# Layer norm roots of a gated FFN kernel split between VectorE and GpSimd, with two moved weight loads and a regrouped LoRA merge

## The chip, the cores and the metric

The kernel runs on 1 core of one Trainium2 chip. The metric is device time in microseconds (us) of one execution. Before the change the median of 3 runs is 442.76 us, from 442.38 to 443.26 us.

## What is computed

The input `u` is 2 x 1024 rows (tokens) of 512 floats; everything is fp32. Each row is normalised (mean and variance over its 512 columns), goes through a state-space convolution over those columns and through a gated FFN with LoRA corrections, and the two results are multiplied and added to the row:

```
def _layernorm(x, axis=-1, eps=1e-05):
    m = jnp.mean(x, axis=axis, keepdims=True)
    v = jnp.var(x, axis=axis, keepdims=True)
    return (x - m) / jnp.sqrt(v + eps)
...
    h1 = _lora_linear(x, w1, lora_A1, lora_B1)
    h3 = _lora_linear(x, w3, lora_A3, lora_B3)
    g = jax.nn.silu(h1) * h3
    return _lora_linear(g, w2, lora_A2, lora_B2)
...
x = L0_attn_u
xn = _layernorm(x, axis=-1)
s = _L0_attn_ref(xn, ...)
g = _silu(_L0_ffn_ref(xn, ...))
x = x + s * g
```

`_lora_linear(x, w, a, b)` is `x w^T + 2 (x a^T) b^T` with rank 16; `w1` and `w3` are 1376 x 512, `w2` is 512 x 1376. Only the layer norm and the first stretch of the first two products (`w1`, `w3`) matter for this change.

## The kernel before

**Blocks.** The 2048 rows are 4 blocks of 512 rows, each of 4 tiles of 128 rows x 512 columns. `load_x` requests the tiles, `norm_stats` takes mean and variance of a tile on VectorE (DVE; `bn_stats` and `bn_aggr`, L247 and L248), `norm_root` computes 1/sqrt(variance + eps) for all tiles of one or two blocks with ten small DVE instructions on a [128, n] tile (L281, the eight of `rsqrt`, L57 to L66, and L284), and `normalize` applies it, one tile after the other, on ScalarE (ACT, L293) or GpSimd (POOL, L297). The tiles are then transposed on TensorE (PE, `transpose`, L304), and ACT copies the results from PSUM into `xr` and `b12` (L312, L314, L315). For block 3 mean and variance come from ACT sums (`act_sums`, `act_squares`, L254 and L265) with small POOL instructions behind them (L260, L261, L274).

**Products.** The products with `w1` and `w3` are done by a scheme of seven products in place of eight, twice nested: on the outside over block pairs, so sums of transposed blocks (`outer_token_sum`, L328, into `xt`) and sums of weights (`outer_weight_sums`, L440) are operands as well. A `Chain` (L765) is seven such products, steps 1, 2, 7, 6, 5, 3, 4. Steps 1, 6, 5 and 3 add into one PSUM bank `x`; after steps 6 and 5 ACT copies the state of that bank away (`snapshot`, L775), and the next step may add to the bank only after the copy. All matmuls of a chain are at L755 (`product`).

The first chain is that of the last 96 hidden rows (`last_chain`, weights `w_last`, tile `last`); the second, beside it, is the first of weight pair 0 (`pair_chain(0, 0)`, weights `w_pair[0]`, tile `w`). Their steps are placed by hand on one time axis with `at(place, what)`; a heap of these events is emptied in order of place, and each engine then runs its own instructions in exactly the order in which they were recorded. So an engine's order is fixed, and an instruction that waits holds everything behind it on its engine. The steps of the first two chains stand at

```
add_chain(0, lambda: last_chain(ab_last, 0),
    ((1, -11), (2, -8), (7, -2), (6, 1.6), (5, 5.6), (3, 8.6), (4, 11.6)))
add_chain(0, pair_chain(0, 0),
    ((1, -4), (2, -1.8), (7, 3.6), (6, 4.6), (5, 7.6), (3, 10.6), (4, 13.6)))
```

**LoRA.** The LoRA term is folded into the weights: `lora_product` (L382) makes a block of it in PSUM by a matmul over 16 rows, `merge` (L392) adds it to the weights on DVE. The LoRA factors lie in groups of 32 partitions of one tile pair (`lo_d`, `lo_h`). `merge_pair` uses groups 0 and 1 and makes four products in two banks, for one half of a pair; it is called twice for pair 0. `merge_whole_pair` uses the four groups and makes all eight products in four banks at once; before the change it serves the later pairs only. The factors of groups 2 and 3 are four small loads (L371, L372).

**Transfers.** All loads except four of the first go out on the sync engine's queue (SP), in program order; a load waits until the one eight places before it has landed. The order is: tiles of block 0, first LoRA factors, block 1, `w1` and `w3` of the last rows (L469), pair 0 (L401), blocks 2 and 3, pair 1, LoRA factors of groups 2 and 3.

**Head and tail.** Before the event list runs, the code records the head: 20 idle matmuls on an identity (`keep_warm`, L990), the LoRA products of the last rows, statistics, root and normalisation of block 0, 5 and 2 more idle matmuls around the transposes of block 0, statistics and root of block 1, and the merges of the last rows. In the list, `normalize(1)` stands at -10, its transposes at -6 and -5, `norm_stats` of block 2 from -6 to -3.6, the root of blocks 2 and 3 at 6.9, `normalize(2)` at 7.3, `normalize(3)` at 7.4, and the transposes of blocks 2 and 3 from 12.1.

Of the kernel before, what the change touches and what calls it, by code (L numbers as in the profile page):

```python
# [17 lines left out]
P = 128  # L18
# [31 lines left out]
def rsqrt(nc, pool, v, shape):  # L50
# [15 lines left out]
    nc.vector.scalar_tensor_tensor(y, t, 5.0, y, ALU.add, ALU.mult)  # L66
    return y
# [40 lines left out]
def s4_gated_ffn(  # L108
# [169 lines left out]
    def norm_root(mv, *blocks):  # L278
        n = len(blocks) * NTT
# [5 lines left out]
        for n, b in enumerate(blocks):  # L285
            norms[b] = [t[:, n * NTT : (n + 1) * NTT] for t in (rstd, shift)]
# [12 lines left out]
    def transpose(b, tiles, tag="aux"):  # L299
        sb, low = divmod(b, 2)  # L300
        for tt in tiles:
            ps = bank(tag)
# [104 lines left out]
    def merge_pair(c, w, half, tag="aux"):  # L407

        ps = [bank(tag), bank(tag)]
        for k in range(2):  # L410
            for v in range(2):
                n = slice(k * 2 * P, (k + 1) * 2 * P)
                lora_product(ps[v][:, n], v, 2 * half + k, PAIR_AT[c], 2 * P, k == 0)
        for v in range(2):
            to = w[:, (1, 2, 0, 3)[2 * v + half]].rearrange("p k m h -> p (k m h)")
            after(1.6 + v, lambda to=to, v=v: merge(to, ps[v]))

# [44 lines left out]
    def load_last():  # L462
# [5 lines left out]
        for v, src in enumerate((w1T, w3T)):  # L468
            nc.sync.dma_start(  # L469
                out=w[:, v], in_=src[:, LAST * P :].rearrange("(dc p) h -> p dc h", p=P)  # L470
            )
        return w, s
# [499 lines left out]
    nc.scalar.activation(warm, warm, AF.Silu)  # L972
    x_in[1] = load_x(1)
    make_upper_triangular(nc, tri, 1.0, diag=True)
    w_last, s_last = load_last()
# [3 lines left out]
    for v, f in enumerate(factors):  # L979
        load_lora(nc.sync, 2 + v, *f, LSPLIT, HID)  # L980
# [19 lines left out]
    for ps in primed:  # L1000
        keep_warm(ps, 10, True)
    ps_last = lora_last()
    mv = norm_tile(0)
    norm_stats(0, range(NTT))
    norm_root(mv, 0)
    normalize(0)

    for i in range(2):
        keep_warm(primed[1], (5, 2)[i])
        transpose(0, range(2 * i, 2 * i + 2))  # L1010
    mv = norm_tile(1)
    norm_stats(1, range(2))
    merge_last(w_last, ps_last, 0)
    norm_stats(1, range(2, NTT))
    norm_root(mv, 1)
    merge_last(w_last, ps_last, 1)
# [41 lines left out]
    at(-10, lambda: normalize(1))  # L1058
# [3 lines left out]
    for i in range(2):  # L1062
        at(-6 + i, lambda i=i: transpose(1, range(2 * i, 2 * i + 2), "y"))
# [529 lines left out]
```

## Time and profile before

| what | us |
|---|---|
| median of 3 runs | 442.76 |
| the profiled execution, its own time | 442.51 |
| its span, first to last instruction | 440.7 |
| PE busy in the span | 434.7 (99%) |
| DVE busy | 315.0 (71%) |
| ACT busy | 144.6 (33%) |
| POOL busy | 209.3 (47%) |

The time holds 1.8 us that lie outside the span (442.51 - 440.7). PE is busy nearly throughout, but its busy time is a model and contains idle matmuls and short waits in the head. The stretches of 5 us from the start show where the engines stand (busy time and, in brackets, the number of instructions):

| stretch | PE | DVE | ACT | POOL | GB/s of DMA |
|---|---|---|---|---|---|
| 0 to 5 | 3.63 (17) | 0.98 (3) | 1.49 (2) | 1.15 (9) | 222 |
| 5 to 10 | 5.00 (43) | 4.31 (17) | 0.34 (1) | 0.28 (1) | 285 |
| 10 to 15 | 5.00 (38) | 4.10 (14) | 3.39 (6) | 1.24 (2) | 349 |
| 15 to 20 | 4.70 (27) | 4.73 (15) | 3.40 (8) | 3.78 (6) | 377 |
| 20 to 25 | 5.00 (21) | 4.33 (9) | 4.49 (14) | 0.36 (2) | 262 |
| 25 to 30 | 4.87 (12) | 4.97 (9) | 4.39 (11) | 0.35 (2) | 10 |
| 30 to 35 | 4.86 (25) | 3.76 (15) | 3.54 (6) | 2.89 (4) | 39 |
| 35 to 40 | 5.00 (24) | 4.96 (7) | 2.60 (6) | 2.25 (4) | 41 |

### The profile page before, as it was taken

How to read it: one execution, taken by the hardware profiler on the slowest of the kernel's cores; microseconds unless marked ns; L12 is line 12 of the kernel's file. 1: busy time of each engine (PE TensorE's matmuls, PEld its weight loads, DVE VectorE, ACT ScalarE, POOL GpSimd, SP SyncE). 2: the span in 40 equal slices, each digit the busy share in tenths (PEclk: the TensorE clock that was granted, in tenths of full speed). 3: DMA queues.
4: the chain of work that ended last, by engine and by line, in shares of the span. 5: the costliest groups of instructions: out<-in, count | busy, mean ns of one | idle time of the engine just before them, and what ended most of it. 6: DMA issues, size and time to landing. Idle time of an engine off the chain costs nothing.

```text
span 440.7 us, 5176 instructions
## 1 busy us (share of the span) xinstructions
PE 434.7 (99%) x1714; PEld 270.7 (61%) x1714; DVE 315.0 (71%) x534; ACT 144.6 (33%) x296; POOL 209.3 (47%) x156
## 2 busy tenths in 40 slices
PE   8999999999999999999999999999999999999996
PEld 8635334444444444444443446888898999999995
DVE  5899999946874687458745796979786885653234
ACT  2776342553245324532453242211101212212221
POOL 2316469995689458936894469400000122222221
PEclk9999999999999999999999999999999999999999
DMA  8921304025002400250045527395901833432211
GB/s 254 369 64 48 123 0 149 24 74 167 25 24 87 153 24 25 92 166 24 25 136 199 162 88 220 98 362 190 348 27 71 304 121 97 143 97 95 84 60 48
DMA packets 35466, 53.61 MB, mean 122 GB/s; under 512 B 4688, under 2 KB 21520, under 8 KB 35312
## 3 DMA queue, kind: packets, MB, share of 16 engines
q1 hardware_dynamic: 35088, 52.69, 36.3%
q10 hardware_dynamic: 352, 0.60, 0.4%
q8 instruction: 13, 0.21, 0.2%
q14 instruction: 13, 0.11, 0.1%
HBM read 33.88 MB, written 19.40 MB: 121 GB/s over the span
## 4 chain that ended last, share of the span: by engine, by line
PE 89%; DMA 4%; DVE 4%; ACT 1%; SPq 1%; issue 1%; ACTq 0%; DVEq 0%
PE x L755 44%; PE y L755 23%; PE w L755 12%; PE aux L929 4%; PE w L929 2%; DMA w<-in_w3T_dram 1%; DMA t_in<-in_x_dram 1%; DMA s<-in_x_dram 1%; DVE xt L328 1%; PE aux L304 1%; PE y L382 1%; PE y L528 1%; PE aux L710 1%; DVE w L440 1%; DMA lo_h<-in_b3T_dram 1%
## 5 line engine op out<-in xcount | busy, mean ns | idle before, releaser
L1311 POOL TENSOR_TENSOR o<-o,xin 128x512 f32<-128x512 f32 (+1 forms) x17 | 23.3, 1370 | 132.8 <-DVE o L1310 127.7
L836 POOL TENSOR_TENSOR s<-c,s 128x512 f32<-128x512 f32 (+1 forms) x44 | 63.6, 1451 | 16.2 <-ACT c L828 11.0
L775 ACT COPY s<-x 128x512 f32<-128x512 f32 (+1 forms) x54 | 31.6, 585 | 87.2 <-PE x L755 87.0
L755 PE MATMUL x<-t_in,s 128*128 128x512 f32 (+1 forms) x148 | 55.2, 500 | 0.0
L779 DVE TENSOR_TENSOR s<-s,y 128x512 f32<-128x512 f32 (+1 forms) x54 | 36.1, 680 | 17.5 <-PE y L755 12.1
L869 POOL TENSOR_TENSOR s<-ua_three,s 128x512 f32<-128x512 f32 x20 | 35.8, 1791 | 25.2 <-DVE s L779 25.2
L755 PEld LDWEIGHTS x<-t_in,s 128*128 128x128 f32 x148 | 26.8, 190 | 22.8 <-issue 12.2
L869 POOL TENSOR_TENSOR ua_three<-ua_three,s 128x512 f32<-128x512 f32 x20 | 33.1, 1653 | 13.8 <-DVE s L779 13.8
L755 PE MATMUL y<-t_in,s 128*128 128x256 f32 (+1 forms) x108 | 35.8, 458 | 0.0
L1333 ACT COPY z<-x 128x256 f32<-128x256 f32 x24 | 8.8, 370 | 70.5 <-PE x L755 70.4
L1308 DVE TENSOR_TENSOR aux<-aux,m 128x384 f32<-128x384 f32 x32 | 18.1, 565 | 15.8 <-PE aux L929 14.2
L869 POOL TENSOR_TENSOR s<-u_three,s 128x512 f32<-128x512 f32 x20 | 28.5, 1427 | 1.8 <-ACT c L828 1.0
L828 ACT ACTIVATE c<-c 128x512 f32<-128x512 f32 x40 | 25.2, 632 | 8.7 <-DVE c L869 8.7
L755 PEld LDWEIGHTS y<-t_in,s 128*128 128x128 f32 x108 | 20.2, 190 | 11.1 <-issue 9.1
L793 ACT COPY w<-x 128x512 f32<-128x512 f32 (+1 forms) x37 | 21.1, 570 | 12.5 <-PE x L755 12.5
L869 POOL TENSOR_TENSOR u_three<-ua_three,u_three 128x512 f32<-128x512 f32 x10 | 15.6, 1557 | 12.8 <-DVE u_three L779 12.7
L755 PE MATMUL x<-t_in,w 128*128 128x512 f32 x40 | 20.9, 603 | 0.0
L755 PE MATMUL x<-xr,w 128*128 128x512 f32 x40 | 20.6, 614 | 0.1
L755 PE MATMUL x<-xt,w 128*128 128x512 f32 x40 | 20.6, 597 | 0.0
L755 PE MATMUL x<-xr,s 128*128 128x512 f32 x40 | 20.6, 616 | 0.0
L755 PE MATMUL x<-xt,s 128*128 128x512 f32 x40 | 20.4, 592 | 0.0
L755 PE MATMUL y<-xt,w 128*128 128x512 f32 x40 | 19.8, 594 | 0.1
(302 smaller groups left out, 908.3 us busy)
## 6 DMA issues: line engine op xcount, KB each, us to landing
g_dram<-s SPq DMA_DIRECT2D x40, 256.0 KB, 2.2
g<-g_dram SPq DMA_DIRECT2D x10, 512.0 KB, 5.9
xin<-in_x_dram SPq DMA_DIRECT2D x16, 256.0 KB, 2.7
out_dram<-o SPq DMA_DIRECT2D x14, 256.0 KB, 2.0
t_in<-g_dram SPq DMA_DIRECT2D x6, 512.0 KB, 4.0
w<-in_w1T_dram SPq DMA_DIRECT2D x10, 256.0 KB, 3.7
w<-in_w3T_dram SPq DMA_DIRECT2D x10, 256.0 KB, 4.7
t_in<-in_x_dram SPq DMA_DIRECT2D x8, 256.0 KB, 5.6
```

The source lines that it names most:

```text
L304: nc.tensor.transpose(ps[:, dc * P : (dc + 1) * P], x_in[b][tt][:, dc * P : (dc + 1) * P], ident,)
L755: nc.tensor.matmul(ps[:, cols], lhsT=lhsT, rhs=rhs if parts == 1 else rhs[:, cols], start=first and i == 0 and part == 0, stop=i == len(pa ...
L775: nc.scalar.copy(t, self.x)
L779: nc.vector.tensor_tensor(t, t, self.y, add)
L793: nc.scalar.copy(self.w, self.x)
L828: nc.scalar.activation(c, c if src is None else src, AF.Silu)
L836: nc.gpsimd.tensor_tensor(g, act, g, mult)
L869: (nc.vector if o < 20 else nc.gpsimd).tensor_tensor(to, a, b, add)
L929: nc.tensor.matmul(to[:, n * P : (n + 1) * P], lhsT=x_, rhs=by, start=start, stop=True, skip_group_check=True,)
L1308: nc.vector.tensor_tensor(y[:, P:], y[:, P:], m[:, n * P : (n + 3) * P], add)
L1311: (nc.vector if last else nc.gpsimd).tensor_tensor(o, o, self.xin[h][:, cols], add)
L1333: nc.scalar.copy(t, xb)
```

## The change

- **Roots.** `rsqrt_on_gpsimd` is new: the same series on POOL, in eleven instructions on a [128, n] tile, each of which reads what the one before wrote. `gp_norm_root` puts one instruction before and two behind it: fourteen in a row. In blocks 0 and 1 the first two tiles' root goes to POOL, the last two's to DVE (`norm_root`, still ten). Blocks 2 and 3 together get one POOL root, at 2 instead of 6.9.
- **Normalisation** of blocks 0 and 1 by halves (`normalize_half`): in block 0 tile 0 on ACT, 1 and 2 on POOL, 3 on DVE; in block 1 tiles 0 and 3 on ACT, 1 and 2 on POOL. Of block 1 the first half stands at -10, the second at -9; the sums of the last weights (`last_sums`, four POOL instructions, L491 to L494 before) stay at -9.9, so between the two. `normalize(3)` moves from 7.4 to 7.7.
- **Idle matmuls**: 9 and 9 instead of 10 and 10, then 4 instead of 5.
- **Transfers**: `w1` of the last rows goes ahead of block 1, `w3` stays behind it, and the four small LoRA loads of groups 2 and 3 go ahead of pair 0.
- **LoRA of pair 0**: one `merge_whole_pair` at -9 with two `y` and two `aux` banks in place of two `merge_pair` (-9 and -3.8).
- **Block 1's transposes**: tile 0 into a borrowed `x` bank, the others into `y`, at -6 and -5.9.
- **Places on DVE**: the statistics of block 2 move from -6 ... -3.6 to -0.25, -0.2, 0.45 and 0.5, and token sum 1 from -1 to -0.45.

```diff
--- before.py
+++ after.py
@@ -64,6 +64,26 @@
     nc.vector.scalar_tensor_tensor(t, t, 1.0 / part**2, v, ALU.mult, ALU.mult)
     nc.vector.scalar_tensor_tensor(t, t, -10.0 / 3.0, t, ALU.add, ALU.mult)
     nc.vector.scalar_tensor_tensor(y, t, 5.0, y, ALU.add, ALU.mult)
+    return y
+
+
+def rsqrt_on_gpsimd(nc, pool, v, shape):
+
+    y = pool.tile(shape, F32, tag="rg_y", name="rg_y")
+    t = pool.tile(shape, F32, tag="rg_t", name="rg_t")
+    u = pool.tile(shape, F32, tag="rg_u", name="rg_u")
+    g, c2 = nc.gpsimd, 0.703952253
+    g.tensor_scalar(y.bitcast(I32), v.bitcast(I32), -0.5, float(0x5F1FFFF9), ALU.mult, ALU.add)
+    g.tensor_tensor(t, y, y, ALU.mult)
+    g.tensor_tensor(t, t, v, ALU.mult)
+    g.tensor_scalar(t, t, -c2, c2 * 2.38924456, ALU.mult, ALU.add)
+    g.tensor_tensor(y, t, y, ALU.mult)
+    g.tensor_tensor(t, y, y, ALU.mult)
+    g.tensor_tensor(t, t, v, ALU.mult)
+    g.tensor_scalar(u, t, 3.0 / 8.0, -10.0 / 8.0, ALU.mult, ALU.add)
+    g.tensor_tensor(t, u, t, ALU.mult)
+    g.tensor_scalar(t, t, 15.0 / 8.0, None, ALU.add)
+    g.tensor_tensor(y, t, y, ALU.mult)
     return y
 
 
@@ -275,15 +295,41 @@
             norms[b][:, :, 1], sums_of_x[b][:, 2, :], 1.0 / DIM, None, mult
         )
 
-    def norm_root(mv, *blocks):
-        n = len(blocks) * NTT
+    def norm_root(mv):
+        n = mv.shape[1]
         veps = small.tile([P, n], F32, tag="veps", name="veps")
         nc.vector.tensor_scalar(veps, mv[:, :, 1], EPS, None, add)
         rstd = rsqrt(nc, small, veps, [P, n])
         shift = small.tile([P, n], F32, tag="shift", name="shift")
         nc.vector.scalar_tensor_tensor(shift, mv[:, :, 0], -1.0, rstd, mult, mult)
-        for n, b in enumerate(blocks):
-            norms[b] = [t[:, n * NTT : (n + 1) * NTT] for t in (rstd, shift)]
+        return rstd, shift
+
+    def gp_norm_root(mv):
+
+        n = mv.shape[1]
+        veps, shift = (
+            upool.tile([P, n], F32, tag=f"gp_{name}", name=name, bufs=1)
+            for name in ("veps", "shift")
+        )
+        nc.gpsimd.tensor_scalar(veps, mv[:, :, 1], EPS, None, add)
+        rstd = rsqrt_on_gpsimd(nc, upool, veps, [P, n])
+        nc.gpsimd.tensor_tensor(shift, mv[:, :, 0], rstd, mult)
+        nc.gpsimd.tensor_scalar(shift, shift, -1.0, None, mult)
+        return rstd, shift
+
+
+    def normalize_half(b, half, root, act, vector=None):
+        rstd, shift = root
+        for i in range(2):
+            t, one = x_in[b][2 * half + i], slice(i, i + 1)
+            if i == vector:
+                nc.vector.tensor_scalar(t, t, rstd[:, one], shift[:, one], mult, add)
+            elif i == act:
+                nc.scalar.activation(
+                    t, t, AF.Identity, bias=shift[:, one], scale=rstd[:, one]
+                )
+            else:
+                nc.gpsimd.tensor_scalar(t, t, rstd[:, one], shift[:, one], mult, add)
 
     def normalize(b, on_act=(0, 2)):
         rstd, shift = norms[b]
@@ -296,10 +342,10 @@
             else:
                 nc.gpsimd.tensor_scalar(t, t, rstd[:, one], shift[:, one], mult, add)
 
-    def transpose(b, tiles, tag="aux"):
+    def transpose(b, tiles, tag="aux", borrow=False):
         sb, low = divmod(b, 2)
         for tt in tiles:
-            ps = bank(tag)
+            ps = bank(tag, borrow)
             for dc in range(NDC):
                 nc.tensor.transpose(
                     ps[:, dc * P : (dc + 1) * P],
@@ -404,17 +450,6 @@
                 )
         return w
 
-    def merge_pair(c, w, half, tag="aux"):
-
...
     def merge_whole_pair(c, w, first=None, delays=(1.15, 2.3, 4.3, 4.4)):
 
         ps = [first or [bank("y", True), bank("w", True)], [bank("aux"), bank("aux")]]
@@ -465,11 +500,14 @@
             both[:, i].rearrange("p (a b h) -> p a b h", a=n, h=LASTR)
             for i, n in enumerate((2, 4))
         )
-        for v, src in enumerate((w1T, w3T)):
+
+        def load(v):
             nc.sync.dma_start(
-                out=w[:, v], in_=src[:, LAST * P :].rearrange("(dc p) h -> p dc h", p=P)
+                out=w[:, v],
+                in_=(w1T, w3T)[v][:, LAST * P :].rearrange("(dc p) h -> p dc h", p=P),
             )
-        return w, s
+
+        return w, s, load
 
     def lora_last():
         ps = [bank("y"), bank("y")]
@@ -970,14 +1008,16 @@
     for v, f in enumerate(factors):
         load_lora((nc.sync, nc.scalar)[v], v, *f, LSPLIT, HID)
     nc.scalar.activation(warm, warm, AF.Silu)
+    w_last, s_last, load_of_last = load_last()
+    load_of_last(0)
     x_in[1] = load_x(1)
+    load_of_last(1)
     make_upper_triangular(nc, tri, 1.0, diag=True)
-    w_last, s_last = load_last()
+    for v, f in enumerate(factors):
+        load_lora(nc.sync, 2 + v, *f, LSPLIT, HID)
     w_pair, s_pair = {0: load_pair(0)}, {c: {} for c in range(NPAIR)}
     x_in[2], x_in[3] = load_x(2), load_x(3)
     w_pair[1] = load_pair(1)
-    for v, f in enumerate(factors):
-        load_lora(nc.sync, 2 + v, *f, LSPLIT, HID)
 
     def other_factors():
         for v, (_, h) in enumerate(factors):
@@ -998,22 +1038,25 @@
 
     primed = bank("w"), bank("w")
     for ps in primed:
-        keep_warm(ps, 10, True)
+        keep_warm(ps, 9, True)
     ps_last = lora_last()
+
+
     mv = norm_tile(0)
-    norm_stats(0, range(NTT))
-    norm_root(mv, 0)
-    normalize(0)
-
-    for i in range(2):
-        keep_warm(primed[1], (5, 2)[i])
-        transpose(0, range(2 * i, 2 * i + 2))
+    for half in range(2):
+        norm_stats(0, range(2 * half, 2 * half + 2))
+        root = (gp_norm_root, norm_root)[half](mv[:, 2 * half : 2 * half + 2])
+        normalize_half(0, half, root, *((0,), (None, 1))[half])
+        keep_warm(primed[1], (4, 2)[half])
+        transpose(0, range(2 * half, 2 * half + 2))
+    merge_last(w_last, ps_last, 0)
     mv = norm_tile(1)
-    norm_stats(1, range(2))
-    merge_last(w_last, ps_last, 0)
-    norm_stats(1, range(2, NTT))
-    norm_root(mv, 1)
-    merge_last(w_last, ps_last, 1)
+    roots = []
+    for half in range(2):
+        norm_stats(1, range(2 * half, 2 * half + 2))
+        if half:
+            merge_last(w_last, ps_last, 1)
+        roots.append((gp_norm_root, norm_root)[half](mv[:, 2 * half : 2 * half + 2]))
     mv_late = norm_tile(2, 3)
     ab_last = last_operands(w_last, s_last)
 
@@ -1055,26 +1098,36 @@
             if (c, n) == (NPAIR - 1, 5):
                 places = (*PLACES[:-1], (4, 13.5))
             add_chain(2 + 7 * c + n, pair_chain(c, n), places)
-    at(-10, lambda: normalize(1))
+    for half in range(2):
+        at(-10 + half, lambda half=half: normalize_half(1, half, roots[half], half))
     at(-9.9, lambda: last_sums(w_last, s_last))
-    at(-9, lambda: merge_pair(0, w_pair[0], 0))
-    at(-3.8, lambda: merge_pair(0, w_pair[0], 1))
-    for i in range(2):
-        at(-6 + i, lambda i=i: transpose(1, range(2 * i, 2 * i + 2), "y"))
+    at(
+        -9,
+        lambda: merge_whole_pair(
+            0, w_pair[0], [bank("y"), bank("y")], (1.6, 1.7, 1.8, 1.9)
+        ),
+    )
+    at(-6, lambda: transpose(1, (0,), "x", True))
+    at(-5.9, lambda: transpose(1, range(1, NTT), "y"))
     for n, name in enumerate((3, 2, 1)):
-        at((-2.3, -1.5, -1)[n], lambda name=name: outer_token_sum(0, name))
+        at((-2.3, -1.5, -0.45)[n], lambda name=name: outer_token_sum(0, name))
         at(-0.6 + 0.3 * n, lambda name=name: outer_weight_sums(w_pair[0], (name,)))
     at(0.4, lambda: outer_token_sum(0, 4))
     at(0.8, lambda: outer_weight_sums(w_pair[0], (4,)))
     for tt in range(NTT):
-        at(-6 + 0.8 * tt, lambda tt=tt: norm_stats(2, (tt,)))
+        at((-0.25, -0.2, 0.45, 0.5)[tt], lambda tt=tt: norm_stats(2, (tt,)))
         at(-1.4 + 0.1 * tt, lambda tt=tt: act_sums(3, tt))
         at((-0.3, -0.2, 1.7, 1.8)[tt], lambda tt=tt: act_squares(3, tt))
     at(-0.9, lambda: act_means(3))
     at(1.9, lambda: act_variances(3))
-    at(6.9, lambda: norm_root(mv_late, 2, 3))
+    def late_root():
+        roots = gp_norm_root(mv_late)
+        for n in range(2):
+            norms[2 + n] = [t[:, n * NTT : (n + 1) * NTT] for t in roots]
+
+    at(2, late_root)
     at(7.3, lambda: normalize(2))
-    at(7.4, lambda: normalize(3, (0,)))
+    at(7.7, lambda: normalize(3, (0,)))
     for n, place in enumerate((12.1, 12.8, 13.7, 14.4)):
         b, i = divmod(n, 2)
         at(place, lambda b=b, i=i: transpose(2 + b, range(2 * i, 2 * i + 2)))
```

More of the change, by code (lines that the diff above doesn't have):

```diff
@@ L405, in load_pair @@
         return w
-    def merge_pair(c, w, half, tag="aux"):
[L409 to L416, printed above, removed]
     def merge_whole_pair(c, w, first=None, delays=(1.15, 2.3, 4.3, 4.4)):
```

## The prediction

> **What bounds the kernel now.** I read the chain of waits first, then the timeline of the first 48 us, engine by engine. From 37.5 us to the end the chain is PE almost alone (the page gives PE 89% of it), so a change in the head is worth what it shifts the first PE instruction of that unbroken stretch. The chain just ahead of it (start, duration, engine and line):
>
> ```profile
> 29.51 0.60 DVE w L440
> 30.11 0.09 DVE veps L281
> ...
> 31.83 0.18 DVE shift L284
> 32.01 0.02 issue
> 32.04 2.23 ACT t_in L293 x3
> 34.26 0.47 ACT ua_three L775
> 34.74 0.04 issue
> 34.78 1.12 PE x L755 x2
> ```
>
> DVE finishes the weight sums, makes the root of blocks 2 and 3 (ten steps, 2.0 us), ACT normalises three tiles, and only then copies the snapshot `ua_three`, which stands behind them in its order; PE's step 3 of pair chain 0 waits for that copy. PE could have begun it at 34.48 (last start 34.05 + 0.43), so the late root costs 0.3 us now. PE's other waits between 11.0 and 34.8 are 0.46 us at 19.38 (a PSUM bank) and 0.29 at 27.12 (a weight sum).
>
> The prices come from these rows of the timeline (start, duration, engine, line, tiles, shape):
>
> ```profile
> 17.56 0.59 POOL L491 TENSOR_TENSOR last<-last 128x192 f32<-128x192 f32 x1
> 18.23 0.59 POOL L492 TENSOR_TENSOR last<-last 128x192 f32<-128x192 f32 x1
> 18.78 0.59 POOL L493 TENSOR_TENSOR last<-last 128x192 f32<-128x192 f32 x1
> 19.33 0.60 POOL L494 TENSOR_TENSOR last<-last 128x192 f32<-128x192 f32 x1
> 24.64 0.23 POOL L260 TENSOR_SCALAR act_sums<-act_sums 128x4 f32<-128x4 f32 x1 [4.71 <-ACT c L254]
> 24.83 0.22 POOL L261 TENSOR_SCALAR mv<-act_sums 128x4 f32<-128x4 f32 x1
> 29.29 0.30 POOL L274 TENSOR_SCALAR mv<-act_sums 128x4 f32<-128x4 f32 x1 [4.23 <-ACT c L265]
> ```
>
> **Price of the POOL root.** A small POOL tensor_scalar starts 0.19 after the one before if it needn't wait for it. Waiting costs 0.12 more: L492 reads what L491 wrote and starts 0.67 after it, L493 and L494 start 0.55 after theirs. So a dependent one is 0.31. A tensor_tensor starts every 0.55 at 192 columns and takes 1.27 at 512 (L836 at 35.84), 2.1 ns a column, which leaves 0.14 at two columns, 0.26 dependent. The root has six of the first kind and eight of the second: 6 x 0.31 + 8 x 0.26 = 3.9 us, against 2.0 on DVE. Bounds: 14 x 0.19 = 2.7 if waiting is free; 14 x 0.38 = 5.3 if each costs the 0.30 of L274 and 0.08 (end of L491 to start of L492).
>
> **Block 0.** POOL starts after the second tile's aggregate (5.69) and ends at 5.8 + 3.9 = 9.7; DVE's root for the other half ends at 9.62 as before. ACT's tile takes 0.81, so the first transpose can start at 10.6; PE, with 36 idle matmuls in place of 40 (0.112 apart, 0.45 less) and 8 in place of 10, is free at 10.3. Before: 10.99. Gain 0.4, and this lead carries to block 1: its transposes come up 7.05 later (18.04 - 10.99), at 17.65. The LoRA regrouping costs nothing there: eight products over four row groups took 1.08 (30.72 to 31.80), four over two took 1.06 (15.18 to 16.25), so the second batch (21.40 to 22.46) is a clean 1.06 saved.
>
> **Transfers.** In flight are eight loads; the order only swaps some. Pair 0 now waits for block 1's tiles (landed up to 11.1 before) instead of the LoRA factors, and comes behind 140 KB more: last piece at about 15.9 instead of 15.43, still ahead of its merges on DVE at 16.2. Block 1 lands 0.6 later per tile (192 KB took 0.58), DVE reaches the third and fourth tile at 12.2 and 13.1, after they landed (about 11.1 and 11.8). Blocks 2 and 3 land before 22, first used after that. Cost nothing; if pair 0 were 1 us later, the merges would slip 0.7.
>
> **Block 1.** DVE: normalises its tile from 9.66, 0.35 to 0.7 (no such row; ACT's is 0.72, POOL's 0.75), merges 0.48, two statistics of 0.82 each: POOL's root starts at 12.4 and ends at 16.3. Behind it on POOL stand, in this order, tile 1 (0.75, to 17.1), `last_sums` (2.37 in the rows above, to 19.5), tile 2 (to 20.2). Tile 2 was ready at 17.59 before. PE has transposed tiles 0 and 1 at 18.5 and waits 1.75 us; the last transpose ends at 21.3, ACT's copies at 22.2 (0.84 after it, as 20.61 to 21.44), and DVE's first token sum starts there, 0.7 later than before (21.48). Step 7 of the last chain starts at 22.95 (22.46 before): the saved 1.06 and the lead of 0.4 are eaten by the late tile.
>
> **DVE's list from there.** Four token sums of two halves and four weight sums at 0.60, four statistics of 0.82 now between them: the last aggregate ends 10.0 after the first sum's start, at 32.2. Before, these statistics ran from 17.56 to 20.85, where DVE had time. PE doesn't mind: 23 + steps 7, 2, 6, 7, 6, 5, LoRA, 5, 3 brings it to 34.6 with no wait for a sum.
>
> **The late root.** So POOL starts the root of blocks 2 and 3 at 32.3, when DVE's root was already done (32.0). The last weight sum runs on DVE from 32.1 to 32.8. What such a sum does to POOL:
>
> ```profile
> 48.55 5.12 POOL L869 TENSOR_TENSOR s<-ua_three,s 128x512 f32<-128x512 f32 x1 [6.04 <-DVE s L779]
> 50.80 1.75 DVE L340 TENSOR_TENSOR t_in<-xr 128x1536 f32<-128x1536 f32 x1
> 52.65 2.63 DVE L342 TENSOR_TENSOR t_in<-t_in,xr 128x1536 f32<-128x1536 f32 x1
> ```
>
> POOL's 1.27 us of work end 1.1 us after DVE's first seam, at 52.55, and DVE's next instruction is 0.9 longer. So I let the root's first step pass at 32.8 and the other 13 take 3.65: 36.5. (The Trainium skill, SBUF — State Buffer, "Who interferes with whom", says the same in general: a DVE instruction with two SBUF inputs and a GpSimd one that reads SBUF exclude each other for a whole instruction. By it every step that meets DVE's own root in blocks 0 and 1 could be held too; the sum by the rows leaves that out, since DVE's steps are 0.16 long, and by the rule it would be up to 1 us longer per root.) ACT waits for this root with its next two tiles, and the snapshot stands behind both: 36.55 + 2 x 0.71 + 0.56 + 0.05 = 38.6. PE, free at 34.6, waits 4.0 us, and step 3 starts at 38.6 instead of 34.78: **+3.8 us**. Moving `normalize(3)` behind the snapshot takes 0.7 out of this; it is in the sum. Nothing behind it absorbs the shift: before, PE has no wait over 0.25 us from 35 to 100 us, and DVE and POOL move along (POOL ends its tiles at 40.3, PE wants the last one at 47).
>
> Sum: span 440.7 + 3.8 = 444.5, and with the 1.8 around it **446.3 us**. The profiled execution (442.51) is 0.25 below the median, so against the median it is +3.5.
>
> **A clock risk.** PE's idle matmuls start 0.21 apart (20 in the 4 us from 2 to 6) and 0.11 apart after 6.9, so PE ran at half rate for its first 5.5 us. No idle stretch of before is over 1 us, so no row says whether 4 us of idling bring the half rate back: 0 to 2.7 us (half of 5.5). I take 0 and keep 2.7 for the range. (TensorE: Matmul & The Clock Gate, "What's actually happening", of the skill throttles after an idle window of some 3.4 us and releases after a busy one; an estimate by that is 0 or 1.7 us.)
>
> **Rivals.**
> - *POOL's cheap end.* At 2.7 us the block 1 root ends at 15.1, tile 2 at 19.0, DVE's sums start at 20.9, the root ends at 33.7, the snapshot at 35.75: +1.0, 443.5. For it: L261's 0.19. Against: L492's wait.
> - *POOL's dear end, or the half rate.* At 5.3 the root ends at 39.4 (block 1 adds 1.4): +6.7, 449.2; the half rate on the forecast gives 449.0.
> - *The other side: POOL's two-column steps nearly free.* The memsets at the start of the program (128x1) start 0.03 apart. At 14 x 0.03 = 0.4 us tile 2 is never late, the sums start at 20.3, the root ends at 31.3, and PE gets its snapshot at 33.4: -1.4, 441.1. At 0.13 a step it is even (the snapshot at 34.78); faster only below that. Against: no POOL row that reads anything starts under 0.19 after its predecessor.
> - *The stall is hidden anyway*, which would take the root ready by 32.7: the statistics end at 30.3 even with no late tile, so it can't be with 2.7 or more.
>
> **How the numbers follow.** Forecast, dear and cheap steps around it (445 to 448): 0.58; cheap end (443.3 to 445): 0.13; dear end or half rate (448 to 450): 0.13; even, 0.06; faster, 0.10. Of the last two I leave out most, and the tip of the dear end: range 443.3 to 449.3. A measurement tells 0.2% (0.89 us) from no change: slower 0.83, the same 0.07, faster 0.10.
>
> **What would show it.** In the profile after: fourteen POOL steps 0.26 to 0.31 apart, three times; tile 2 of block 1 behind the four weight sums on POOL, ending near 20.2; the late root from 32 to 36.5; the longest PE wait of the head ended by ACT's `ua_three` copy near 38.6; PE unbroken after it. Wrong if POOL's steps are under 0.15 apart, if the statistics of block 2 end before 29, or if PE doesn't wait for that copy.

## The result, and the profile after

The changed kernel takes 447.54 us (median of 4 runs, 447.21 to 448.42); the kernel before took 442.64 beside it (4 runs, 442.38 to 443.26). The ratio is 1.0109, with a 95% interval of 1.0097 to 1.0121: slower by about 4.9 us. The profiled execution of the changed kernel took 448.42 us, the slowest of its four, with a span of 446.6 and a mean granted clock of 0.992; the other three had 0.995 or 0.996.

Line numbers shift with the change. The product is now L793 (L755 before), the copy of the snapshot L813 (L775), VectorE's total of it L817 (L779), a token sum L374 (L328), a weight sum of two 512-wide pieces L475 (L440), one of 896 columns L487 (L452), a merge L438 (L392), a LoRA product L428 (L382), the normalizing of whole blocks L339 on ACT and L343 on POOL, of halves L328 and L332, and GpSimd's root L314, L76 to L86, L316, L317.

The chain of waits of the changed kernel answers to the first fence of the prediction (start, duration, engine and line):

```profile
31.94 0.19 DVE mv L268
...
32.28 0.54 POOL veps L314
...
36.33 0.25 POOL shift L317
...
37.33 0.80 ACT t_in L339
38.13 0.48 ACT ua_three L813
38.61 0.04 issue
38.65 2.08 PE x L793 x2
40.73 3.31 PE y L793 x4
44.03 0.87 PE aux L350 x8
```

The root's ten DVE steps have become fourteen POOL steps, from 32.28 to 36.58; the snapshot still stands behind two normalized tiles on ACT, and step 3 starts at 38.65 where it had started at 34.78: 3.87 us later. One thing more is new: four matmuls took 3.31 us, where four took 1.72 before.

POOL's timeline for block 1 (start, duration, engine, line, operation, tiles, shape) shows the price of a small step and what is queued behind the root:

```profile
12.30 0.22 POOL L314 TENSOR_SCALAR veps<-mv 128x2 f32<-128x2 f32 x1 [0.76 <-DVE mv L268]
12.61 0.19 POOL L76 TENSOR_SCALAR rg_y<-veps 128x2 int32<-128x2 int32 x1
12.89 0.19 POOL L77 TENSOR_TENSOR rg_t<-rg_y 128x2 f32<-128x2 f32 x1
...
15.97 0.22 POOL L317 TENSOR_SCALAR shift<-shift 128x2 f32<-128x2 f32 x1
16.29 0.77 POOL L332 TENSOR_SCALAR s<-s,rg_y,shift 128x512 f32<-128x512 f32 x1
17.02 0.59 POOL L529 TENSOR_TENSOR last<-last 128x192 f32<-128x192 f32 x1
...
19.38 0.78 POOL L332 TENSOR_SCALAR s<-s,rs_y,shift 128x512 f32<-128x512 f32 x1
```

A dependent step starts some 0.28 us after the one before it, tensor_scalar and tensor_tensor alike, and the root takes 3.9 us. Tile 2's normalizing (the last line) waits behind the four sums of the last weights, as its place in POOL's order says, although its own root came from DVE.

PE's timeline at the wait has two things in it, the wait and the rate after it:

```profile
38.65 2.08 PE L793 MATMUL x<-xr,w 128*128 128x512 f32 x2 [3.89 <-ACT ua_three L813]
40.52 3.52 PE L793 MATMUL y<-xt,last 128*96 128x512 f32 x4
43.87 1.04 PE L350 MATMUL aux<-ident,t_in 128*128 128x128 f32 x8
```

PE waited 3.89 us, and the six matmuls that start from 38.65 to 43.1 then come some 0.85 us apart instead of 0.43: half the rate. The granted clock says the same: read in stretches of 0.1 us, it falls to a half at 36.97, inside the wait, and is back at 43.80. At the transposes behind them PE is 6.41 us late (43.87 against 37.46), 2.54 more than at step 3.

DVE stands in its own order behind the snapshot as well:

```profile
38.63 0.69 DVE L817 TENSOR_TENSOR ua_three<-ua_three,y 128x512 f32<-128x512 f32 x1 [4.14 <-ACT ua_three L813]
39.23 1.28 DVE L438 SCALAR_TENSOR_TENSOR w<-aux,w 128x512 f32<-128x512 f32 x2
40.43 2.21 DVE L487 TENSOR_TENSOR s<-w 128x896 f32<-128x896 f32 x1
```

It waits 4.14 us for the copy (0.94 before), and the first 896-wide sum then takes 2.21 us (1.50 before). POOL's product with the gate (L874) starts at 40.43 too.

### The profile page after: what moved, and what is told of

Same layout as the page of the kernel before. It is cut to its first block, busy times and chain, and to the rows that moved or that the text cites. A ratio compares the mean times of both kernels' runs of the same rounds, so it can differ in the third digit from the quotient of the medians.

```text
span 446.6 us, 5201 instructions
## 1 busy us (share of the span) xinstructions
PE 435.0 (97%) x1708; PEld 269.9 (60%) x1708; DVE 314.3 (70%) x525; ACT 143.6 (32%) x295; POOL 215.0 (48%) x198
## 3 DMA queue, kind: packets, MB, share of 16 engines
HBM read 33.88 MB, written 19.40 MB: 119 GB/s over the span
## 4 chain that ended last, share of the span: by engine, by line
PE 90%; DVE 4%; POOL 3%; issue 1%; DMA 1%; ACT 1%; POOLq 0%; DVEq 0%; ACTq 0%
PE x L793 45%; PE y L793 24%; PE w L793 12%; PE aux L967 4%; PE w L967 2%; DVE xt L374 1%; DVE stats L267 1%; PE aux L350 1%; DMA s<-in_x_dram 1%; POOL s L332 1%; PE y L428 1%; PE y L566 1%; PE aux L748 1%; DVE aux L1361 0%; DVE w L475 0%
## 5 line engine op out<-in xcount | busy, mean ns | idle before, releaser
L874 POOL TENSOR_TENSOR s<-c,s 128x512 f32<-128x512 f32 (+1 forms) x44 | 63.2, 1441 | 17.1 <-ACT c L866 11.5
L813 ACT COPY s<-x 128x512 f32<-128x512 f32 (+1 forms) x54 | 31.6, 585 | 87.8 <-PE x L793 87.7
L793 PE MATMUL x<-t_in,s 128*128 128x512 f32 (+1 forms) x148 | 55.2, 500 | 0.0
L817 DVE TENSOR_TENSOR s<-s,y 128x512 f32<-128x512 f32 (+1 forms) x54 | 36.1, 680 | 17.9 <-PE y L793 12.3
L907 POOL TENSOR_TENSOR s<-ua_three,s 128x512 f32<-128x512 f32 x20 | 32.4, 1618 | 31.3 <-DVE s L817 31.3
L793 PEld LDWEIGHTS x<-t_in,s 128*128 128x128 f32 x148 | 26.8, 190 | 22.8 <-issue 12.2
L793 PE MATMUL y<-t_in,s 128*128 128x256 f32 (+1 forms) x108 | 35.8, 458 | 0.0
L793 PEld LDWEIGHTS y<-t_in,s 128*128 128x128 f32 x108 | 20.1, 190 | 11.2 <-issue 8.8
L793 PE MATMUL x<-xr,w 128*128 128x512 f32 x40 | 21.6, 639 | 3.9 <-ACT ua_three L813 3.9
L793 PE MATMUL x<-t_in,w 128*128 128x512 f32 x40 | 20.8, 603 | 0.0
L793 PE MATMUL x<-xt,w 128*128 128x512 f32 x40 | 20.6, 597 | 0.0
L793 PE MATMUL x<-xr,s 128*128 128x512 f32 x40 | 20.5, 613 | 0.0
L793 PE MATMUL x<-xt,s 128*128 128x512 f32 x40 | 20.4, 592 | 0.0
L793 PE MATMUL y<-xt,s 128*128 128x512 f32 x40 | 19.9, 595 | 0.0
```

What stands on the lines that cost most here:

```text
L793: nc.tensor.matmul(ps[:, cols], lhsT=lhsT, rhs=rhs if parts == 1 else rhs[:, cols], start=first and i == 0 and part == 0, stop=i == len(pa ...
L813: nc.scalar.copy(t, self.x)
L817: nc.vector.tensor_tensor(t, t, self.y, add)
L874: nc.gpsimd.tensor_tensor(g, act, g, mult)
L907: (nc.vector if o < 20 else nc.gpsimd).tensor_tensor(to, a, b, add)
```

## The experiments

Three questions were open. Is the late root on POOL the loss, or the order around it? How much does the half rate cost? And is PE, as the prediction said, the engine whose lateness sets the end, or is it DVE? All twelve kernels are variants of the changed one unless something else is said. Times are medians; "before" is the kernel before on the same chip.

**e1, the late root back on DVE.**

```diff
-        roots = gp_norm_root(mv_late)
+        roots = norm_root(mv_late)
```

> Only the root of blocks 2 and 3 goes back to VectorE, at the same place (2); everything else as in the changed kernel. Theory (the root is late because its statistics end at 32.1, and ScalarE's snapshot stands behind it; GpSimd's 4.3 us against VectorE's 2.0 is only part of it): the root runs from 32.6 to 34.6, the snapshot ends at 36.7, PE waits 2.1 us instead of 4.0, and the matmuls after the wait keep the full rate. Shift against the kernel before at that place +1.9, minus the 0.5 that is absorbed later: about 444.2 us. Rival A (GpSimd's roots as such are the whole loss): back to 442.6. Rival B (the late tile 2 of block 1 is the loss): no change, 447.5.

Measured: 445.88 us, ratio 1.0072 (1.0057 to 1.0087). That is a third of the loss. DVE's root ran from 33.31 to 35.29 us, as quick as before but 3.3 us later, because the statistics of block 2 still stand between the token sums, and step 3 came at 37.36. In this profiled execution a tile of block 0 also landed 0.56 us later than in the changed kernel's. So the engine of the late root is not the whole cause: its late start is as much.

**e2, the snapshot ahead of the normalizing on ACT.**

```diff
-    at(7.3, lambda: normalize(2))
+    at(7.65, lambda: normalize(2))
```

> Only the normalisation of block 2 moves from place 7.3 to 7.65, that is behind ScalarE's snapshot; the GpSimd root stays as late as it is. Theory: PE's step 3 starts at 34.6 with no wait, the transposes of block 2 begin at 37.5 when the tiles are there, and ScalarE's activation and copies behind the normalised tiles cost PE two smaller waits of about 1 us and 0.3 us near 38.4 and 40.3; no idle stretch over 1.5 us, so no half rate. Shift +1.2 at 40 us, about 443.6 us. Rival (PE needs the normalised tiles themselves, not the snapshot): the wait only moves to the transposes, 3 us or more stay, over 445.5.

Measured: 449.30 us, ratio 1.0152 (1.0136 to 1.0167): a miss of almost 6 us, and the most instructive run. Step 3 started at 34.44 with no wait, as meant. But DVE, no longer held behind the snapshot, went on to the 896-wide weight sums. DVE's timeline of this kernel:

```profile
36.04 1.08 DVE L487 TENSOR_TENSOR s<-w 128x896 f32<-128x896 f32 x1
37.16 1.09 DVE L487 TENSOR_TENSOR s<-s,w 128x896 f32<-128x896 f32 x1
38.16 0.68 DVE L817 TENSOR_TENSOR s<-s,y 96x512 f32<-96x512 f32 x1
38.76 1.08 DVE L487 TENSOR_TENSOR s<-w,s 128x896 f32<-128x896 f32 x1
```

And POOL's, in the same stretch:

```profile
35.30 0.24 POOL L85 TENSOR_SCALAR rg_t<-rg_t 128x8 f32<-128x8 f32 x1
35.63 1.55 POOL L86 TENSOR_TENSOR rg_y<-rg_t,rg_y 128x8 f32<-128x8 f32 x1
37.26 1.05 POOL L316 TENSOR_TENSOR shift<-mv,rg_y 128x8 f32<-128x8 f32 x1
38.40 2.16 POOL L317 TENSOR_SCALAR shift<-shift 128x8 f32<-128x8 f32 x1
40.66 4.19 POOL L343 TENSOR_SCALAR t_in<-t_in,rg_y,shift 128x512 f32<-128x512 f32 x5
```

Three steps of 0.20 to 0.25 us, on eight columns, took 1.55, 1.05 and 2.16: the first two end 0.06 us after a DVE sum of 896 columns (37.18 and 38.31, the sums at 37.12 and 38.25), and the last gets through only after the third such sum and into the 512-wide ones behind it (40.55). The root ended at 40.56 instead of 36.58, and PE waited 4.3 us at the transposes, for tiles that nobody had normalized yet. Half rate followed here too, in the granted clock from 40.9 to 47.7, so not all of the miss is the root. So DVE's wait at the snapshot had been a shelter for POOL's root. The Trainium skill states this kind of block (SBUF — State Buffer, "Who interferes with whom": a DVE instruction with two SBUF inputs contends with a GpSimd one that reads SBUF, and the port pair that they share is an exclusive lock). These rows agree with it.

**e3, the wait filled with idle matmuls**, so that PE doesn't stand still.

```diff
+    at(10.5, lambda: keep_warm(bank("w", True), 18, True))
```

> The changed kernel with 18 idle matmuls (36 passes, 4.0 us at full rate) recorded on PE just ahead of step 3 of pair chain 0, so that PE works through its wait. Theory (the matmuls from 38.65 to 43.1 took 0.853 in place of 0.429 because PE had been idle for 4 us): they take 0.43, step 3 still starts at 38.7, and the time falls by 2.5 to about 445.0 us. Rival (the half rate comes from something else, for example a fixed moment, or ScalarE and GpSimd traffic): unchanged at 447.5 or longer.

PE's timeline of this kernel:

```profile
34.67 4.18 PE L1030 MATMUL w<-ident 128*128 128x128 f32 x36
38.73 1.13 PE L793 MATMUL x<-xr,w 128*128 128x512 f32 x2
39.70 1.88 PE L793 MATMUL y<-xt,last 128*96 128x512 f32 x4
```

The half rate is gone: six matmuls in 2.85 us instead of 5.4. Yet the time is 447.11 us, ratio 1.0102 (1.0085 to 1.0119): 0.4 us won at the median. Between the two profiled executions it is 1.3 (spans 445.3 and 446.6) of the 2.54 that PE had lost in the changed kernel's; in that kernel's other three executions the mean clock was higher, and what PE lost in them is not on record. Behind the wait PE's shift no longer jumps, but it creeps from 3.95 us at step 3 to 4.4 at 62, 4.7 at 74 and 4.9 at 315. The chain of waits tells why: in the changed kernel it is PE from 38.65 us on, in this one DVE, which adds the snapshot 3.95 us late and begins its long token sum (L388) 4.67 us late. Without the half rate DVE is the later of the two, so half of the half rate or more was covered.

**e4, tile 2 of block 1 ahead of the last sums on POOL.**

```diff
-    at(-9.9, lambda: last_sums(w_last, s_last))
+    at(-8.9, lambda: last_sums(w_last, s_last))
```

> Only the four GpSimd sums of the last weights move behind the tile 2 of block 1 (place -9.9 to -8.9). Theory: that tile is ready at 17.8 instead of 20.15, PE's wait of 1.6 us at 18.6 goes, VectorE's first token sum starts at 20.4 instead of 22.1, the late root ends at about 34.9, and all after it is 1.6 to 1.7 us earlier; PE still waits about 4 us for the snapshot and has the half rate after it: about 445.9 us. Rival (the late tile is covered by the later wait): no change, 447.5.

Measured: 446.20 us, ratio 1.0082 (1.0067 to 1.0097). Tile 2 was normalized by 18.55 instead of 20.15, DVE's first token sum came 0.8 us earlier, and 1.3 us of time came with it. In the profiled execution PE waited 3.90 us for the snapshot, one hundredth more than in the changed kernel, and this time the matmuls behind it ran at the full rate (mean clock 1.000, 446.21 us). The other three executions had a mean clock of 0.995 or 0.996 and took 446.10, 446.19 and 446.85, so here no price of the lower clock can be told. The snapshot came only 0.78 us earlier than in the changed kernel; a tile of block 0 landed 0.5 us later here, as in e1.

**e5, e1 and e2 and e4 together.**

> The late root goes back to DVE, the snapshot stands ahead of the last blocks' normalizing on ACT, and GpSimd takes block 1's tile 2 before it makes the last sums. If the loss comes from the late root's time on GpSimd and from what DVE's sums do to it, then TensorE waits less than 0.5 us at product step 3, which starts at 33.1 to 34.0 (34.78 in the kernel before, 38.65 in the changed one), and less than 1 us at the transposes behind it; the time is about 441.5. Rival: VectorE, which has the root's 2 us back on its list beside the weight sums, is late instead and TensorE waits for it between 50 and 65 us; then 442.7 or more. If the slow root was never the cause, the time stays near 446.

Measured: 444.26 us, ratio 1.0034 (1.0020 to 1.0049). Step 3 started at 33.82, almost a microsecond before that of the kernel before, and still the time is 1.6 us over it: the rival's line. The chain of waits runs on DVE from 34 us to the end of the head; some of its pieces:

```profile
34.04 0.68 DVE w L438
34.72 0.59 DVE s L817
35.31 0.60 DVE ua_three L817
...
38.14 1.54 DVE s L487
...
41.77 1.70 DVE w L475
...
53.77 2.63 DVE t_in L388
```

PE, with no wait over 0.25 us from 35 to 100 us in the kernel before, waits 0.5 and 0.4 us for DVE here.

**e7, no root on POOL at all**: e2 with the roots of blocks 0 and 1 made whole on DVE, block 1's ahead of its merge, and the late one too.

> No root is on GpSimd and no block's normalizing is halved; of the change only the LoRA products four at a time, the loads and the order of weights are left, with the snapshot ahead of the last normalizing. If the roots on GpSimd are the whole loss, this is at or under the kernel before: about 441.7 from the 1.06 us that the LoRA products give, within 0.5 of e5. If the regrouped LoRA products or the loads lose time too, it is over 443.

Measured: 444.84 us, ratio 1.0047 (1.0032 to 1.0062). POOL's roots are not the whole loss: the expectation's first branch fell. Step 3 is on time here (34.69) but DVE is not: its root ends at 34.6, and it adds the snapshot at 36.35 instead of 34.76. The second branch, that the loads lose time too, stays open: in this profiled execution PE's LoRA products waited for what the profile names a load until 15.90 us (they ran on from 14.91 in e5), and DVE's first token sum started at 22.23 against e5's 21.05.

**e8, only the statistics of the late root earlier**, two of them in DVE's idle time ahead of block 1's first token sum.

```diff
-        at((-0.25, -0.2, 0.45, 0.5)[tt], lambda tt=tt: norm_stats(2, (tt,)))
+        at((-3, -2.9, -0.25, -0.2)[tt], lambda tt=tt: norm_stats(2, (tt,)))
```

> The changed kernel, but with the four statistics of the late root earlier: two in VectorE's idle time near 20 us, two ahead of product step 1. The root then starts at about 30 to 31 instead of 32.3 and ends by 34.8 instead of 36.6; product step 3 starts at 36.9 or earlier, 1.75 before that of the changed kernel, TensorE's wait there is about 2.3 us instead of 4.1 and its clock stays at full rate: about 445.5. Rival: the root is still held by VectorE's sums and ends near 36.5 whatever its start; then 447.3.

Measured: 445.48 us, ratio 1.0067 (1.0052 to 1.0083), as expected, though the parts were 0.4 off: the root ran from 30.86 to 35.18 and step 3 started at 37.26, after a wait of 2.2 us and at full rate. The start of the root is worth 2 us of the 4.9, or 1.6 against e3, which kept its rate too.

**e6, e8 with e2 and e4.**

> The late root stays on GpSimd, but two of its four statistics are made some 8 us earlier, in VectorE's idle time before block 1's first token sum, the others ahead of product step 1; the snapshot stands ahead of the normalizing and tile 2 ahead of the last sums. If the loss is a matter of when the root starts, and of VectorE's long sums from SBUF holding the root's small steps, the root now runs from about 30 to 34 us, before those sums, and TensorE waits nowhere for 1 us between 33 and 48: about 441.7. Rival: GpSimd's steps are held at whatever time they run because VectorE always has some sum to make; then the root ends after 36 and the time is 444 or more.

Measured: 441.97 us, ratio 0.9992 (0.9982 to 1.0001). With the root early enough, POOL's root is done (35.27 in the profiled execution) before the first of DVE's 896-wide sums (35.96), and the whole loss is gone with all three roots still on POOL. Whether it is faster than the kernel before can't be told from the interval.

**e9, e6 with one early statistic in place of two.**

```diff
-        at((-3, -2.9, -0.25, -0.2)[tt], lambda tt=tt: norm_stats(2, (tt,)))
+        at((-3, -0.3, -0.25, -0.2)[tt], lambda tt=tt: norm_stats(2, (tt,)))
```

> As the kernel with two early statistics, the snapshot and tile 2 first, but with one early statistic only. In that kernel VectorE had no idle time from 18.7 to 31 us and its second early statistic held block 1's first token sum by 0.75 us. If VectorE's list sets the end, the first sum and everything behind it come 0.75 us earlier: VectorE adds the snapshot at about 33.4 instead of 34.16 and the time is about 441.2 instead of 441.97. Rival: what follows waits for ACT or TensorE anyway, and the time stays at 442.0.

Measured: 442.23 us, ratio 0.9992 (0.9983 to 1.0002): no gain over e6. The early part of the expectation came true, the late part didn't. DVE's timeline:

```profile
33.09 0.68 DVE L817 TENSOR_TENSOR ua_three<-ua_three,y 128x512 f32<-128x512 f32 x1
33.68 1.28 DVE L438 SCALAR_TENSOR_TENSOR w<-aux,w 128x512 f32<-128x512 f32 x2
34.88 1.33 DVE L487 TENSOR_TENSOR s<-w 128x896 f32<-128x896 f32 x1
36.24 1.55 DVE L487 TENSOR_TENSOR s<-s,w 128x896 f32<-128x896 f32 x1
```

And POOL's:

```profile
34.50 7.25 POOL L343 TENSOR_SCALAR t_in<-t_in,rg_y,shift 128x512 f32<-128x512 f32 x5
41.71 3.39 POOL L874 TENSOR_TENSOR s<-c,s 96x512 f32<-96x512 f32 x2
```

DVE adds the snapshot 1.68 us earlier than in the kernel before, and then gives it back: its sums now run beside POOL's five tiles, which take 7.25 us instead of 3.78, and each holds the other. At the long token sum it is only 0.23 us ahead. (The gap of 0.75 us that the expectation names was read from e6's profiled execution, which was the slowest of its ten, so it was a poor row to read it from.)

**e10, e9 with the LoRA products of pair 0 in two batches again**, as in the kernel before.

```diff
-    at(-9, lambda: merge_whole_pair(0, w_pair[0],
-        [bank("y"), bank("y")], (1.6, 1.7, 1.8, 1.9)))
+    at(-9, lambda: merge_pair(0, w_pair[0], 0))
+    at(-3.8, lambda: merge_pair(0, w_pair[0], 1))
```

> The kernel with one early statistic, the LoRA products of pair 0 again in two batches as in the kernel before. If making them four at a time is worth the 1.06 us that the prediction gives it on TensorE, this takes 0.7 to 1.1 us longer than that kernel. Rival: VectorE, not TensorE, is the bound in that stretch, and the two agree within 0.3.

Measured: 443.63 us, 1.40 over e9 (the two ratios, 1.0019 with 1.0010 to 1.0028 and 0.9992, don't overlap) and more than the 0.7 to 1.1 expected. But TensorE reaches step 3 at 33.75, no later than in e9 (33.88). DVE's timeline now has two merges between the token sums:

```profile
20.96 1.29 DVE L374 TENSOR_TENSOR xt<-xr,b 128x512 f32<-128x512 f32 x2 [0.97 <-ACT xr L361]
22.20 0.69 DVE L438 SCALAR_TENSOR_TENSOR w<-aux,w 128x512 f32<-128x512 f32 x1
22.81 1.28 DVE L374 TENSOR_TENSOR xt<-xt,xr 128x512 f32<-128x512 f32 x2
24.01 0.68 DVE L438 SCALAR_TENSOR_TENSOR w<-aux,w 128x512 f32<-128x512 f32 x1
```

DVE adds the snapshot 0.5 us later than in e9 (33.61 against 33.09). Where the rest goes, the chain of waits shows:

```profile
34.98 8.75 POOL t_in L343 x5
...
43.78 0.67 PE aux L350 x4
...
44.47 0.37 ACT b L360
```

POOL's five tiles take 8.74 us instead of e9's 7.25; PE waits 0.93 us for the last of them, and DVE, which by 43.09 was 0.8 us ahead of e9, waits 1.39 us for ACT's copies of it. So making the products four at a time is worth somewhat more than the prediction gave it, but not by what PE saves: the loss comes out at POOL's tiles. That the two merges, 1.2 us among the token sums, make DVE's sums meet those tiles in another way is argued, not shown.

**e11, the kernel before with one thing changed: the late root on POOL**, at its old place.

```diff
-    at(6.9, lambda: norm_root(mv_late, 2, 3))
+    at(6.9, lambda: gp_norm_root(mv_late, 2, 3))
```

> The kernel before with one thing changed: the root of blocks 2 and 3 is made on GpSimd, at its old place. The root runs from 30.1 to about 34.2 us instead of 30.1 to 32.0, so ACT makes the snapshot 2.2 us later, TensorE's step 3 starts at about 37.0 instead of 34.78, and VectorE adds the snapshot that much later: 444.8 to 445.3, some 2.2 to 2.7 over the kernel before. Rival: VectorE, which has 2 us less to do, makes up for it: within 0.5 of the kernel before.

Measured: 445.47 us, ratio 1.0053 (1.0040 to 1.0067), 2.6 over the kernel before: the size is the one expected, and the rival fell. The root ran from 29.57 to 33.87. PE's timeline (here the product is L788, the snapshot L808):

```profile
36.65 2.05 PE L788 MATMUL x<-xr,w 128*128 128x512 f32 x2 [2.10 <-ACT ua_three L808]
38.50 2.69 PE L788 MATMUL y<-xt,last 128*96 128x512 f32 x4
```

Here a wait of 2.10 us is followed by the half rate, until 40.1. The six runs fall in two groups: four with a mean clock of 0.995 or 0.996 took 445.41 to 445.84, two with 0.999 or 1.000 took 444.06 and 444.12. So of the 2.6 us some 1.4 go with the half rate, which the expectation didn't have, and 1.2 to 1.3 are the root: that the sum came out is luck.

**e12, e9 with all four tiles of block 2 normalized on ACT**, and none of block 3, so one tile fewer on POOL.

```diff
-    at(7.65, lambda: normalize(2))
-    at(7.7, lambda: normalize(3, (0,)))
+    at(7.65, lambda: normalize(2, (0, 1, 2, 3)))
+    at(7.7, lambda: normalize(3, ()))
```

> The kernel with one early statistic, in which VectorE was 1.68 us ahead of the kernel before at the snapshot and only 0.23 ahead at 59 us, GpSimd's normalizing meanwhile taking 1.2 to 2.1 us a tile instead of 0.75. Here ACT normalizes all four tiles of block 2 and GpSimd the four of block 3, so one tile fewer on GpSimd. If it is these tiles that hold VectorE's sums, about 0.45 us of the lost 1.45 comes back: 441.8 instead of 442.2, with at most half of it if TensorE has to wait for ACT's later copies. Rival: the loss has another source, or the sums meet the remaining tiles as long: 442.2 or more.

Measured: 442.43 us, ratio 0.9999 (0.9988 to 1.0011): nothing. POOL's four tiles took 0.77, 1.60, 1.59 and 2.13 us, and then its products with the gate came a tile earlier and met the sums in the fifth tile's stead (1.70 and 1.71 us). The same number of POOL's instructions was held; the rival's second half, that the sums meet the remaining work as long, fits these rows.

**All fourteen kernels side by side.** Each number is from the profiled execution, as a difference to the kernel before (34.78, 34.76, 59.20 and 440.7 us): when PE starts step 3, when DVE adds the snapshot, when DVE starts its long token sum (`t_in<-t_in,xt`, 2048 columns), and the span.

| kernel | PE, step 3 | DVE, snapshot | DVE, long sum | span |
|---|---|---|---|---|
| changed | +3.87 | +3.87 | +5.91 | +5.9 |
| e1 late root on DVE | +2.58 | +2.58 | +3.29 | +3.5 |
| e2 copy first | -0.34 | -0.51 | +6.74 | +6.6 |
| e3 wait filled | +3.95 | +3.95 | +4.67 | +4.6 |
| e4 tile first | +3.09 | +3.09 | +3.81 | +3.6 |
| e5 = e1, e2, e4 | -0.96 | +0.47 | +1.12 | +1.3 |
| e6 = e8, e2, e4 | +0.17 | -0.60 | +0.66 | +0.8 |
| e7 no POOL roots | -0.09 | +1.59 | +2.23 | +2.5 |
| e8 early statistics | +2.48 | +2.48 | +3.20 | +2.9 |
| e9 one early statistic | -0.90 | -1.68 | -0.23 | -0.4 |
| e10 e9, LoRA in halves | -1.03 | -1.15 | +0.86 | +0.7 |
| e11 before, late POOL root | +1.87 | +1.87 | +3.05 | +2.8 |
| e12 e9, block 2 on ACT | -1.01 | -1.79 | -0.34 | -0.2 |

The span follows DVE's long sum within 0.3 us in every row; PE's step 3 misses it by 0.4 us in the best row and by 6.9 in the worst. The long sum lies 24 us behind step 3, and by then PE's lag has become DVE's: PE's product `x<-xr,s` near 70 us (69.76 in the kernel before) is 1.12 us late in e5 and 4.67 in e3, and in e9 0.23 early. Two engines run side by side here with hardly any idle time, and the later one sets the end. Where PE lost time to the half rate, in the changed kernel, e2 and e11, the chain of waits after 39 us is PE's but for what ends the wait, and DVE waits for what PE makes. From DVE's waits after 39 us in the changed kernel (engine, line, what it waited for, us in total, times, longest):

```profile
DVE ua_three L817 <- ACT ua_three L813: 4.1, 1, 4.1
DVE u_three L817 <- ACT u_three L813: 0.6, 1, 0.6
DVE xt L374 <- ACT xr L361: 0.4, 1, 0.4
DVE s L817 <- PE y L793: 0.3, 1, 0.3
```

In the profiled executions whose clock stayed up the chain of the same stretch is mostly DVE's (e1, e3, e4, e5, e8 and e9 among them; in e10 POOL's tiles stand ahead of it), and e5 and e7 separate the two plainly: PE early or on time, DVE late, and the time is DVE's. No kernel delayed DVE alone with nothing else changed, so that it is the cause rests on those rows and chains, not on a run made for it.

## Why the prediction was right, and where it was off

**The price of the POOL root: right.** It was put at 3.9 us from fourteen steps of 0.26 to 0.31; the steps start 0.27 to 0.31 apart and the root of block 1 took 3.89 (12.30 to 16.19). That the sum came out exactly is partly luck: it took the two kinds of step to differ, 0.31 and 0.26, and they don't at this size. The steps that run beside DVE's own root in blocks 0 and 1 were not held (0.19 to 0.24 us).

**Block 0 and block 1: right.** First transpose at 10.64 (10.6 predicted), tile 2 done at 20.16 (20.2), PE's wait 1.6 us (1.75; counted by starts, as the prediction does, where the profile's row has 1.41), first token sum at 22.13 (22.2), step 7 of the last chain at 22.97 (22.95), last aggregate at 32.12 (32.2). e4 confirms that tile 2 behind the last sums is what cost it: 1.3 us.

**The late root: right.** Its first step was held by the weight sum until 32.81 (32.8 predicted), it ended at 36.58 (36.5), and step 3 started at 38.65 (38.6). e11 shows the root alone, without the late statistics, at 1.2 to 1.3 us at the full clock and 2.6 with the half rate; e8 shows what part of the statistics' lateness costs, 2.1.

**The transfers: wrong, and harmless in this kernel.** Pair 0's last piece landed at 17.53, not at 15.9; the second merge waited until 17.65 and DVE had the time. In e7 a load may have counted.

**The LoRA products: right in size, wrong in place.** The saved 1.06 us were counted on PE. e10 shows 1.40 at the median, with PE's arrival at step 3 unchanged: there it is lost at POOL's tiles and in DVE's wait for the last of them.

**"Nothing behind it absorbs the shift ... DVE and POOL move along": this step failed, in both directions.** They don't move along rigidly. DVE came out of its wait 3.87 us late and met POOL's work otherwise than before, so that a sum of 1.50 us took 2.21. In e3, where PE kept its rate, DVE lost another 0.7 us between the snapshot and its long sum, and e1, e4, e5, e7 and e8 lose 0.6 to 0.7 in the same stretch. That term, 0.7, was missing from the sum. And something does absorb: the two lags, PE's and DVE's, run side by side, and only the larger one counts. That a sum made on PE alone came near is in part luck: DVE waits for the same copy as PE and came out of it just as late, 3.87 us.

**The clock: the half rate came, and its size was missed twice.** It was taken as 0, with 2.7 us kept as a bound. On PE it cost 2.54 in the profiled execution, close to the bound. At the end it was worth 0.4 at the median (447.54 less e3's 447.11) and 1.3 between the profiled executions, because DVE would have been late without it. In e11, where DVE loses less, it was worth some 1.4. The prediction's first sentence, that a change in the head is worth what it shifts PE, was read from a chain that names PE for every stretch in which PE was busy. DVE was full in the same stretch of the kernel before (14.90 of 15 us from 48 to 63), and the chain didn't show it, since neither waited for the other.

So the measured 4.9 us are about 3.87 at step 3, 0.7 that DVE lost on the way to its long sum, and 0.4 for the half rate, against a forecast of 3.5 to 3.8; in the profiled execution the last term is 1.3 and the sum 5.9. The rivals of a cheap root and of nearly free steps fell with the first row of the root; the half rate was a rival that came true and counted for little, 0.4 of 4.9 at the median.

## What to carry to other kernels

When two engines are both full over a stretch, the chain of waits names one of them, and a gain on that one may be worth nothing: look at which other engine has no idle time there, and ask how late each comes out of the change. Small steps on POOL were cheap here while DVE waited, made statistics or merged from PSUM (12 to 16 and 33 to 36.5 us in the changed kernel), and dear while it added from SBUF; so place such a root with that in view, and before taking away a wait of DVE's look at what POOL does under its cover. What an engine stands behind in its own order (tile 2 behind four sums, statistics between token sums, the snapshot behind two tiles) cost as much here as the operations that were moved.

## What the runs showed of the hardware

- POOL: a dependent two- or eight-column step takes 0.19 to 0.25 us and starts 0.27 to 0.33 after the one before. Beside a DVE sum of 512 columns it took 0.47 to 0.55 (e9 and e10, 30 to 32 us), beside sums of 896 up to 2.16 (e2).
- The half rate after a wait doesn't follow from the wait's length alone. Waits of 3.89 us in the changed kernel, 4.28 in e2 and 2.10 in e11 were followed by it in the profiled executions; 3.90 in e4's, 2.23 in e8's and 1.90 in e1's were not. In the changed kernel and in e11 the granted clock fell 2.2 us after PE's last product had ended (34.76 to 36.97, 34.55 to 36.71), in e2 3.7 us after (37.18 to 40.9). The Trainium skill (TensorE: Matmul & The Clock Gate, "What's actually happening") has the clock fall after about 3.4 us of idleness, in a window that runs freely. That the same wait goes both ways agrees with a window of free phase; that 2.2 us were enough doesn't agree with an idle window of 3.4.
- Once it was there, it lasted 6.8 us in the changed kernel and in e2 (36.97 to 43.80, 40.9 to 47.7) and 3.4 in e11 (36.71 to 40.12); PE was at work in 5.1, 6.3 and 3.4 us of that.
